# A graph layer on one core: 66 message buffers, one fetched tile in 36 split over two queues, three copies moved from ScalarE to VectorE, wider second tiles, and the last groups' products over fewer tiles

## The chip, the core and the metric

The kernel runs on one core of a Trainium2 chip. A core has TensorE (PE, whose loading of weights is shown as PEld), VectorE (DVE), ScalarE (ACT), GpSimd (POOL) and SyncE (SP), each with its own queue of instructions, and 16 DMA engines that all queues share. The metric is the device time of one execution in microseconds; lower is better. Most executions agree within 0.3%.

## What is computed

A graph of 12500 nodes with 256 features, and 212500 edges sorted by destination, each with a source, a destination and one of eight types. Node features are normalised and clipped at zero; each edge carries its source's features, multiplied by the weight of its type; messages are added up at their destination.

```
h = maximum(layernorm(x), 0)                        # 12500 x 256
hx = einsum('ni,rio->rno', h, weight)               # 8 types
agg = segment_sum(hx[edge_type, src], dst, 12500)
x + agg * sqrt(0.5) + h_bias + (h @ loop_weight) * sqrt(0.5)
```

Every node also has an edge to itself in the list. All values are float32.

## The kernel before

The kernel adds up first and multiplies after: for each destination node and type it sums the features `h` of the sources (`acc`), and then multiplies the sums of 128 nodes (a group, 98 in all) by the eight weights.

Edges are worked in *units*, 802 of them, each of two *tiles* of up to 128 edges, 1603 tiles in all. The first 128 units take 256 edges, later ones 267: the last edge of a node is its self edge where it appears so, and is left out of the tiles and added by the group's own path (`begin`, below). Block b is 128 units, whose indices are prepared together on VectorE.

For each tile t:

- `gather` (L742 to L760) fills a message buffer `msg[t]` (128 edges x 256) by an indirect DMA of POOL, one source row per partition. It is called 58 tiles (`AHEAD`) before the tile is used, into a ring of 60 buffers (`MSGS`). The first 96 tiles are gathered from `x`, while `h` is still being made, and are normalised in place: `moments` on DVE, and a pass of ACT (L716). The others are gathered from `h` in DRAM (`h32`).
- After block 0, one tile in 48 (`SINGLE`) is not gathered by POOL. `load_sources` (L762 to L773) loads 16 row addresses at a time into SP's registers (L765), and SP issues one DMA per row of 1 KB (L770). These steps stand in a list `fetches`, from which `fetch` takes four (`FETCH`) per tile, from eight tiles (`HOLD`) after the call on.
- `onehots` (L779) makes, for four tiles at a time, a 128 x 176 matrix per tile that says which of 22 nodes x 8 types an edge belongs to (L788). It runs 8 tiles (`LEAD`) ahead.
- `edge_sums` (L806) multiplies messages and one-hots on PE into one of four PSUM banks (L821): the first tile of a pair by 176 columns, the second, whose nodes are known to lie among the first 13 (`REACH`), by 104. In the profile each such product appears as two matmuls, so a tile has four.
- `add_sums` (L831) adds the bank of the pair before (L835, DVE) into a window of 22 nodes of `acc`, a ring of six groups of 128 nodes.

When a group's sums are complete (`plan.last`, worked out in `Plan` from bounds on where a unit's nodes can lie), its 18 products enter a queue that spreads them over the tiles up to `until`, at most some 16 tiles (L1012, 36 matmuls in the profile). `finish` (L1021) adds bias and products to the rows of x (L1024, L1025, DVE), and SP stores the rows for four groups at once (L1030), for the last two singly (L1027). SP also loads rows of x and h (L962).

The features of a group's own nodes are transposed on PE (L862) and copied by ACT to `self_t` (L867). For groups 12 and later `begin` writes them into `acc` by type (L884, eight DVE operations), and ACT's copy waits until these are done. The type of each node's self edge is found for four groups at once by `find_types`: ACT makes a diagonal matrix in four passes (L937), PE spreads it, ACT copies the result (L948).

The order of every engine is written out by the loop over tiles in `tile_preln_rgcn_kernel`: at tile t each step issues its instructions, and each engine runs its own in that order, waiting on semaphores. SP's stores and row fetches stand in one queue in that order.

Of the kernel before, what the change touches and what calls it, by code (L numbers as in the profile page):

```python
# [19 lines left out]
DVE = mybir.EngineType.DVE  # L20
SP = mybir.EngineType.SP

P = 128
# [11 lines left out]
WIN = 22  # L35
REACH = ((0, 13), (0, 22))

# [5 lines left out]

MSGS = 60
AHEAD = 58

SINGLE = 48
FETCH = 4
SOURCES = 16
HOLD = 8  # L50


QUAD = 4
LEAD = 8
PAIR = 2
# [4 lines left out]
DELAY = 6  # L60
REST = 3

BATCH = 4
# [16 lines left out]
class Plan:  # L80
# [7 lines left out]
    def __init__(self, N, E):  # L88
        U = PAIR * P
        first = P * U  # L90
        self.NU = NU = -(-E // U) if E <= first else P + -(-(E - first) // EDGES)
        self.EU = E - (NU - 1) * U if E <= first else E - first - (NU - P - 1) * EDGES
        self.NT = NU * PAIR - (1 if self.EU <= P else 0)
        self.rate = N / E * EDGES
        s = 6.5 * (E / 4) ** 0.5 + EDGES

        lines = [(U, 0), (EDGES, first - P * EDGES)]
        last = (1.1 * EDGES, 1.1 * (first - P * EDGES) - 0.1 * E - 1.5 * EDGES + s)
        self.low = [(a * N / E, (b - s) * N / E) for a, b in [*lines, last]]
# [16 lines left out]
        self.typed = min([q for q, b in enumerate(self.blocks) if b], default=len(self.blocks))  # L116
        assert XG * self.typed >= SLOTS
# [102 lines left out]
def kernel(  # L220
# [61 lines left out]
    with ExitStack() as main:  # L282
# [31 lines left out]
        added, zeroed = {}, {}  # L314
        single, fetches = {}, []
        state = {"h32": None}
# [425 lines left out]
        def gather(t):  # L742
# [18 lines left out]

        def load_sources(t, r0):  # L762

            b, _, u = place_of(t)
            _, vals = nc.values_load_multi_w_load_instructions(  # L765
                single[b][u : u + 1, r0 : r0 + SOURCES], engines=[SP],
                min_val=0, max_val=(N - 1) * D * 4,
                skip_runtime_bounds_check_because="clamped to the table where they are computed")
            for i, v in reversed(list(enumerate(vals))):
                fetches.insert(0, (0, lambda i=i, v=v: nc.sync.dma_start(  # L770
                    msg[t][r0 + i : r0 + i + 1, :].bitcast(U8),
                    h32_bytes[:, bass.ds(v, D * 4)])))
# [80 lines left out]

        def turn_nodes(g, pool, written=None):

# [9 lines left out]
            def keep():  # L865
                got["self", g] = pool.tile([P, KC, GROUP], F32, name="self_t")
                i = nc.scalar.activation(got["self", g][:, :, :n], pst[:, :, :n], AF.Copy)  # L867
                if written:
                    tc.add_manual_dep(
                        i.ins, written[0].name, SYNC_DEP, reason="one reader at a time")  # L870

            return turn, keep, pst

        def begin(g):

            n = plan.ends[g] - plan.starts[g]
            q, k = divmod(g, XG)
            written = []
            turn, keep, pst = turn_nodes(g, selves, written)
            s0 = g % SLOTS * GROUP  # L880

            def own(r):
                of = typed[q][:, k * GROUP : k * GROUP + n].unsqueeze(1).to_broadcast([P, KC, n])
                i = nc.vector.scalar_tensor_tensor(  # L884
                    acc[:, :, r, s0 : s0 + n], of, float(r + 1), pst[:, :, :n],
                    op0=ALU.is_equal, op1=ALU.mult)
                if r == R - 1:
                    zeroed[g, "slot"] = i.ins
                    written.append(i.ins)

# [19 lines left out]
        def find_types(q):  # L910
# [11 lines left out]
            def kinds_of():  # L922
# [11 lines left out]
                nc.vector.tensor_reduce(kinds, one, AX.X, ALU.add)  # L934
                marked[q] = marks.tile([P, XG * GROUP], BF16, name="diagonal")
# [32 lines left out]
        def group_ahead(g):  # L968
# [88 lines left out]
        with tc.manual_schedule():  # L1057
# [56 lines left out]
            def scale_weights():  # L1114
                for o in outs:
                    i = nc.vector.tensor_copy(o[:, 1, :], bias_in)
                done["bias"] = i.ins.name
# [41 lines left out]
            for t in range(NT):  # L1159
# [113 lines left out]
```

## Time and profile before

| | us |
|---|---|
| median of 3 runs (2019.54 to 2027.53) | 2020.34 |
| profiled execution | 2021.12 |
| its span | 2019.4 |
| PE busy / PEld / DVE | 1776.1 / 1585.9 / 1318.5 |
| ACT / POOL | 218.5 / 1497.1 |
| mean granted clock of PE | 0.951 |

A profile is one execution. "Busy" is the time in which an engine runs instructions; a group's line gives the count, the busy time, the mean of one in ns, and the idle time before its instructions with what ended it ("issue": nothing that the profile shows). In a timeline each line has the start, the duration, and in brackets the idle time before. In a view by stretch, the columns are the stretch, its length, the busy time of PE, PEld, DVE, ACT and POOL with counts, the granted clock, the DMA engines' busy share, and GB/s. In a view of one line the three durations are the least, the median and the greatest in ns. "SPq" and "ACTq" are the issuing queues of SP and ACT, whose DMA and register instructions do not count as busy.

### The profile page before, as it was taken

What the parts mean: (1) busy time and instruction counts of PE and PEld (TensorE: products, weight loads), DVE (VectorE), ACT (ScalarE), POOL (GpSimd) and SP (SyncE); (2) the same over time, 40 slices, a digit from 0 to 9 for tenths busy, and PEclk for the clock granted to TensorE, in tenths of its full rate; (3) what the DMA queues carried; (4) which work ended last, traced back from release to release, by engine and by line L of the source; (5) the groups of instructions that cost most, each with busy time, mean ns of one, the idle gap of its engine ahead of it and who ended that gap; (6) DMA issues with size and microseconds to landing.
All of it is one profiled execution on the core that took longest, in us unless ns stands there. A gap on an engine that the chain in (4) does not pass through costs nothing.

```text
span 2019.4 us, 36387 instructions
## 1 busy us (share of the span) xinstructions
PE 1776.1 (88%) x10411; PEld 1585.9 (79%) x10411; DVE 1318.5 (65%) x3282; ACT 218.5 (11%) x470; POOL 1497.1 (74%) x1602
## 2 busy tenths in 40 slices
PE   2458999998998898999998998898998898988998
PEld 2357999997888888888777777787787787877886
DVE  7869667687665578656577655578565568665642
ACT  7844110000000000000000000000000000000000
POOL 7757777777777777777777777777777777777773
PEclk8569999998999999999999999999999999999999
DMA  8963443444444444444444444444444444444442
GB/s 296 378 219 100 148 137 106 128 144 122 128 140 120 139 137 119 128 118 139 130 126 139 128 125 134 129 127 140 128 118 139 127 122 129 119 139 122 118 121 70
DMA packets 152577, 281.63 MB, mean 139 GB/s; under 512 B 31149, under 2 KB 101940, under 8 KB 152372
## 3 DMA queue, kind: packets, MB, share of 16 engines
q0 software_dynamic: 75648, 206.67, 34.6%
q1 hardware_dynamic: 76724, 72.61, 11.3%
q8 instruction: 82, 1.34, 0.3%
q14 instruction: 123, 1.01, 0.2%
HBM read 253.55 MB, written 25.60 MB: 138 GB/s over the span
## 4 chain that ended last, share of the span: by engine, by line
PE 36%; DMA 19%; SPq 15%; issue 13%; POOL 8%; DVE 5%; ACT 2%; DVEq 0%; ACTq 0%; POOLq 0%
PE ps L821 19%; PE po L1012 17%; DMA msg<-h,gidx 14%; SPq L770 11%; POOL msg L758 8%; SPq L765 3%; ACT xt L716 1%; DMA h<-xt 1%; DMA hr<-h 1%; DMA msg<-h 1%; DVE e_stats L704 1%; DVE acc L835 1%; DMA w<-in_L_gnn_weight_dram 1%; DVE oh L788 1%; DMA xr<-in_x_dram 1%
## 5 line engine op out<-in xcount | busy, mean ns | idle before, releaser
L758 POOL DMA_INDIRECT msg<-h,gidx x1480 | 1404.0, 949 | 464.9 <-issue 365.4
L821 PE MATMUL ps<-oh,msg 128*128 128x176 f32 (+1 forms) x6412 | 1127.6, 305 | 219.3 <-DMA msg<-h,gidx 88.3
L821 PEld LDWEIGHTS ps<-oh,msg 128*128 128x128 f32 x6412 | 1023.4, 197 | 377.5 <-DMA msg<-h,gidx 175.6
L1012 PE MATMUL po<-w,acc 128*128 128x256 f32 x3136 | 901.5, 390 | 0.7 <-DVE acc L835 0.7
L835 DVE TENSOR_TENSOR acc<-acc,ps 128x352 f32 x802 | 415.4, 518 | 496.2 <-PE ps L821 490.0
L1012 PEld LDWEIGHTS po<-w,acc 128*128 128x128 f32 x3136 | 538.1, 194 | 24.0 <-DVE acc L835 1.3
L788 DVE TENSOR_TENSOR oh<-fixed,cols 128x704 f32<-128x704 f32 x402 | 353.4, 880 | 0.0
L884 DVE SCALAR_TENSOR_TENSOR acc<-types,pt 128x256 f32<-128x256 bf16 (+1 forms) x688 | 249.4, 413 | 84.3 <-PE pt L862 79.3
L867 ACT ACTIVATE self_t<-pt 128x256 f32<-128x256 f32 x98 | 37.5, 383 | 1456.2 <-DVE acc L884 1387.8
L758 POOL DMA_INDIRECT msg<-in_x_dram,gidx x96 | 91.1, 949 | 31.0 <-issue 25.0
L1012 PE MATMUL po<-wl,self_t 128*128 128x256 f32 x392 | 107.8, 399 | 6.5 <-ACT self_t L867 2.6
L1012 PEld LDWEIGHTS po<-wl,self_t 128*128 128x128 f32 x392 | 70.0, 199 | 13.3 <-ACT self_t L867 3.0
L1024 DVE TENSOR_TENSOR xr<-xr,po 128x256 f32<-128x256 f32 x98 | 40.5, 413 | 18.2 <-PE po L1012 16.7
L716 ACT ACTIVATE xt<-xt,n_shift,n_rstd 128x256 f32<-128x256 f32 x98 | 50.9, 588 | 8.9 <-DVE n_shift L713 8.9
L716 ACT ACTIVATE msg<-msg,e_shift,e_rstd 128x256 f32<-128x256 f32 x96 | 49.6, 588 | 12.9 <-DVE e_shift L713 12.9
L1025 DVE TENSOR_TENSOR xr<-xr,po 128x256 f32<-128x256 f32 x98 | 41.2, 421 | 3.4
L937 ACT ACTIVATE diagonal<-ident,kinds 128x128 bf16<-128x128 f32 x88 | 28.1, 390 | 135.2 <-DVE kinds L934 130.7
L862 PE MATMUL pt<-ident,hr 128*128 128x128 f32 x196 | 38.4, 279 | 0.0
L371 DVE TENSOR_SCALAR moves<-fixed 128x267 int32<-128x267 int32 x84 | 36.0, 429 | 1.1
L704 DVE BATCH_NORM_STATS2 n_stats<-xt 128x6 f32<-128x256 f32 x98 | 34.4, 412 | 2.9 <-DMA xt<-in_x_dram 2.1
L372 DVE COPY_PREDICATED fixed<-moves,fixed 128x266 int32<-128x266 int32 (+6 forms) x84 | 33.7, 401 | 2.9
L704 DVE BATCH_NORM_STATS2 e_stats<-msg 128x6 f32<-128x256 f32 x96 | 33.5, 411 | 0.0
(201 smaller groups left out, 321.1 us busy)
## 6 DMA issues: line engine op xcount, KB each, us to landing
msg<-h SPq DMA_DIRECT2D x3456, 1.0 KB
msg<-h,gidx POOLq DMA_INDIRECT x1480
xt<-in_x_dram SPq DMA_DIRECT2D x24, 512.0 KB
h<-xt SPq DMA_DIRECT2D x24, 512.0 KB
xr<-in_x_dram SPq DMA_DIRECT2D x24, 512.0 KB
hr<-h SPq DMA_DIRECT2D x24, 512.0 KB
out_dram<-xr SPq DMA_DIRECT2D x24, 512.0 KB
w<-in_L_gnn_weight_dram SPq DMA_DIRECT2D x2, 1024.0 KB
```

The lines of the kernel that those rows point to most:

```text
L704: nc.vector.bn_stats(stats[:n, j, :], rows_[j])
L716: nc.scalar.activation(rows_[j], rows_[j], AF.Relu, bias=shift[:n, j : j + 1], scale=rstd[:n, j : j + 1])
L758: nc.gpsimd.indirect_dma_start(out=msg[t], out_offset=None, in_=table[:, :], in_offset=bass.IndirectOffsetOnAxis(ap=gidx[b][:, at : at + 1 ...
L765: _, vals = nc.values_load_multi_w_load_instructions(single[b][u : u + 1, r0 : r0 + SOURCES], engines=[SP], min_val=0, max_val=(N - 1) * D ...
L770: fetches.insert(0, (0, lambda i=i, v=v: nc.sync.dma_start(msg[t][r0 + i : r0 + i + 1, :].bitcast(U8), h32_bytes[:, bass.ds(v, D * 4)])))
L788: j = nc.vector.tensor_tensor(o[:, k : k + v, :i, :], iota_f.unsqueeze(1).unsqueeze(1).to_broadcast([P, v, i, C]), of.unsqueeze(3).to_broa ...
L821: j = nc.tensor.matmul(ps[:, c, :width], m[:, c * P : (c + 1) * P], o[:, :width], start=(i == 0 and c == 0), stop=(end and c == KC - 1))
L835: i = nc.vector.tensor_tensor(a, a, ps, op=ALU.add)
L884: i = nc.vector.scalar_tensor_tensor(acc[:, :, r, s0 : s0 + n], of, float(r + 1), pst[:, :, :n], op0=ALU.is_equal, op1=ALU.mult)
L1012: i = nc.tensor.matmul(got["out", g][:n], lhs, rhs, start=(r == R and c == 0), stop=(r == R - 1 and c == KC - 1))
L1024: nc.vector.tensor_add(rows_[:n, k, :], rows_[:n, k, :], outs[g % 2][:n, 1, :])
L1025: nc.vector.tensor_add(rows_[:n, k, :], rows_[:n, k, :], got["out", g][:n])
```

## The change

- The ring of message buffers has 66 instead of 60, and `AHEAD` is 64. Space for it comes from the bias (now in a row buffer), from two instead of three buffers of columns, and from one buffer of one-hots less.
- `LEAD` is 4 instead of 8: one-hots are made four tiles ahead.
- One tile in 36 is fetched row by row. Its rows 0 to 31 are issued by SP, the other 96 by ACT's queue; each loads 32 addresses at a time. Each engine has its own list, and three steps per tile are taken from each.
- The copies `self_t` and `types`, and the diagonal (now one operation), go to VectorE. The copy of `self_t` no longer waits for `begin`'s writes by a dependency, as one engine does both.
- The second tile of a pair covers 16 nodes, so 128 columns.
- The bound near the end of the edge list is another line, by which groups 84 to 96 count as complete one to three units earlier; the last eight groups (`SOON`) spread their products over at most six tiles (`DELAY`).

In the changed kernel POOL has 1568 gathers, of which 100 are from `x`; ACT has 3360 row DMAs and 105 loads of addresses, SP 1120 and 35.

```
-REACH = ((0, 13), (0, 22))
+REACH = ((0, 16), (0, 22))
-MSGS = 60
-AHEAD = 58
-
-SINGLE = 48
-FETCH = 4
-SOURCES = 16
+MSGS = 66
+AHEAD = 64
+
+SINGLE = 36
+FETCH = 3
+SOURCES = 32
-LEAD = 8
+LEAD = 4
+SOON = 8
-        last = (1.1 * EDGES, 1.1 * (first - P * EDGES) - 0.1 * E - 1.5 * EDGES + s)
+        last = (1.05 * EDGES, 1.05 * (first - P * EDGES) - 0.05 * E - 0.8 * EDGES + s)
-    bias_in = const.tile([P, D], F32, name="bias_in")
-        cols = main.enter_context(tc.tile_pool(name="cols", bufs=3))
+        cols = main.enter_context(tc.tile_pool(name="cols", bufs=2))
-        single, fetches = {}, []
+        single, fetches = {}, {SP: [], ACT: []}
...
-            if b and t % PAIR and kind[t] == "h" and t % SINGLE == SINGLE - 1 and t + AHEAD < NT:
-                for r in range(0, P, SOURCES):
-                    fetches.append((done["tile"] + HOLD, lambda r=r: load_sources(t, r)))
-                return
+            if b and t % PAIR and kind[t] == "h" and t + AHEAD < NT:
+                if t % SINGLE == SINGLE - 1:
+                    for k, r in enumerate(range(0, P, SOURCES)):
+                        engine = ACT if k else SP
+                        fetches[engine].append((
+                            done["tile"] + HOLD,
+                            lambda r=r, engine=engine: load_sources(t, r, engine)))
+                    return
...
-                single[b][u : u + 1, r0 : r0 + SOURCES], engines=[SP],
+                single[b][u : u + 1, r0 : r0 + SOURCES], engines=[engine],
...
+            queue = {SP: nc.sync, ACT: nc.scalar}[engine]
             for i, v in reversed(list(enumerate(vals))):
-                fetches.insert(0, (0, lambda i=i, v=v: nc.sync.dma_start(
+                fetches[engine].insert(0, (0, lambda i=i, v=v: queue.dma_start(
...
-            for _ in range(n):
-                if fetches and fetches[0][0] <= done["tile"]:
-                    fetches.pop(0)[1]()
+            for list_ in fetches.values():
+                for _ in range(n):
+                    if list_ and list_[0][0] <= done["tile"]:
+                        list_.pop(0)[1]()
...
-                i = nc.scalar.activation(got["self", g][:, :, :n], pst[:, :, :n], AF.Copy)
-                if written:
-                    tc.add_manual_dep(
-                        i.ins, written[0].name, SYNC_DEP, reason="one reader at a time")
+                nc.vector.tensor_copy(got["self", g][:, :, :n], pst[:, :, :n])
...
-                for g in range(XG):
-                    nc.scalar.activation(
-                        marked[q][:, g * GROUP : (g + 1) * GROUP], ident, AF.Copy,
-                        scale=kinds[:, g : g + 1])
+                nc.vector.tensor_tensor(
+                    marked[q].rearrange("p (g k) -> p g k", g=XG),
+                    ident.unsqueeze(1).to_broadcast([P, XG, GROUP]),
+                    kinds.unsqueeze(2).to_broadcast([P, XG, GROUP]), op=ALU.mult)
...
-                nc.scalar.activation(typed[q], pt, AF.Copy)
-
-            shared(spread, [(1, types_of)], lambda: q in marked, wait=2)
+                nc.vector.tensor_copy(typed[q], pt)
+
+            shared(spread, [(2, types_of)], lambda: q in marked, wait=2)
...
-                    shared(turn, [(1, keep)])
+                    shared(turn, [(2, keep)])
...
+                bias_in = got["bias"] = rowp.tile([P, XG, D], F32, tag="rows", name="biasr")[:, 0, :]
...
+                        if g >= plan.NG - SOON:
+                            until = min(until, ready + DELAY)
```

More of the change, by code (lines that the diff above doesn't have):

```diff
@@ L21 @@
 SP = mybir.EngineType.SP
+ACT = mybir.EngineType.Activation
 P = 128
@@ L760, in gather, with load_sources @@
                 in_offset=bass.IndirectOffsetOnAxis(ap=gidx[b][:, at : at + 1], axis=0))
-        def load_sources(t, r0):
+        def load_sources(t, r0, engine):
             b, _, u = place_of(t)
             _, vals = nc.values_load_multi_w_load_instructions(
-                single[b][u : u + 1, r0 : r0 + SOURCES], engines=[SP],
+                single[b][u : u + 1, r0 : r0 + SOURCES], engines=[engine],
                 min_val=0, max_val=(N - 1) * D * 4,
                 skip_runtime_bounds_check_because="clamped to the table where they are computed")
+            queue = {SP: nc.sync, ACT: nc.scalar}[engine]
             for i, v in reversed(list(enumerate(vals))):
-                fetches.insert(0, (0, lambda i=i, v=v: nc.sync.dma_start(
+                fetches[engine].insert(0, (0, lambda i=i, v=v: queue.dma_start(
                     msg[t][r0 + i : r0 + i + 1, :].bitcast(U8),
@@ L852, in clear, with turn_nodes @@
             zeroed[g, "slot"] = i.ins
-        def turn_nodes(g, pool, written=None):
+        def turn_nodes(g, pool):
             n = plan.ends[g] - plan.starts[g]
@@ L877, in begin @@
             q, k = divmod(g, XG)
-            written = []
-            turn, keep, pst = turn_nodes(g, selves, written)
+            turn, keep, pst = turn_nodes(g, selves)
             s0 = g % SLOTS * GROUP
@@ L888, in own @@
                     zeroed[g, "slot"] = i.ins
-                    written.append(i.ins)
             def write():
@@ L934, in kinds_of @@
                 nc.vector.tensor_reduce(kinds, one, AX.X, ALU.add)
-                marked[q] = marks.tile([P, XG * GROUP], BF16, name="diagonal")
-                for g in range(XG):
-                    nc.scalar.activation(
-                        marked[q][:, g * GROUP : (g + 1) * GROUP], ident, AF.Copy,
-                        scale=kinds[:, g : g + 1])
+                marked[q] = marks.tile(
+                    [P, 2, XG * GROUP], BF16, tag="mark0", name="diagonal")[:, 0, :]
+                nc.vector.tensor_tensor(
+                    marked[q].rearrange("p (g k) -> p g k", g=XG),
+                    ident.unsqueeze(1).to_broadcast([P, XG, GROUP]),
+                    kinds.unsqueeze(2).to_broadcast([P, XG, GROUP]), op=ALU.mult)
             shared(find, [(2, kinds_of)])
@@ L1115, in scale_weights @@
                 for o in outs:
-                    i = nc.vector.tensor_copy(o[:, 1, :], bias_in)
+                    i = nc.vector.tensor_copy(o[:, 1, :], got["bias"])
                 done["bias"] = i.ins.name
```

## The prediction

> **What bounds the kernel now.** The page's busy shares come first: PE 88%, POOL 74%, DVE 65%. A share doesn't say which engine sets the pace, so the second view is POOL's timeline. The instructions that gather message tiles are on L758.
>
> ```profile
> PE 1776.1 (88%) x10411; PEld 1585.9 (79%) x10411; DVE 1318.5 (65%) x3282; ACT 218.5 (11%) x470; POOL 1497.1 (74%) x1602
> L758 POOL DMA_INDIRECT msg<-h,gidx x1480 | 1404.0, 949 | 464.9 <-issue 365.4
> L758 POOL DMA_INDIRECT msg<-in_x_dram,gidx x96 | 91.1, 949 | 31.0 <-issue 25.0
> ```
>
> ```profile
> 4.72 1.11 POOL L758 DMA_INDIRECT msg<-in_x_dram,gidx  x1 [2.08 <-DVE bound_o L1088]
> ...
> 128.86 0.94 POOL L758 DMA_INDIRECT msg<-h,gidx  x1 [0.30 <-issue]
> 134.98 0.94 POOL L758 DMA_INDIRECT msg<-h,gidx  x1 [5.18 <-ACT e_rstd L708]
> 136.23 0.95 POOL L758 DMA_INDIRECT msg<-h,gidx  x1 [0.30 <-issue]
> 142.96 0.94 POOL L758 DMA_INDIRECT msg<-h,gidx  x1 [5.79 <-issue]
> ...
> 188.83 0.94 POOL L758 DMA_INDIRECT msg<-h,gidx  x1 [2.73 <-issue]
> ...
> 1992.75 0.95 POOL L758 DMA_INDIRECT msg<-h,gidx  x1 [0.30 <-PE ps L821]
> ```
>
> A gather takes 0.95 us and the next follows 0.30 us later, whoever is named as releaser: 1.25 us each. From 4.72 to 1992.75 there are 1576; 1575 x 1.25 = 1969 of the 1988 us. About 13.7 us of the rest are stalls at 129 to 195 us (5.18, 5.79, 1.02, 2.73, 0.49, each less the usual 0.30). So POOL's chain of gathers sets the time, and 26.6 us follow the last one's start. The chain of waits names PE and SPq before 947 us, but POOL's gaps stay at 0.30 there, so I go by the gaps.
>
> Third, busy time by stretch, columns PE, PEld, DVE, ACT, POOL:
>
> ```profile
> 300.00:350.00 50.00, 50.00 (x325) 47.27 (x325) 34.62 (x76) 4.18 (x11) 37.82 (x41) 1.00 0.37 106
> 550.00:600.00 50.00, 46.44 (x291) 43.33 (x290) 30.63 (x66) 3.03 (x8) 37.85 (x40) 0.97 0.45 131
> 750.00:800.00 50.00, 46.49 (x297) 43.41 (x295) 43.87 (x116) 2.64 (x7) 37.81 (x41) 0.99 0.42 122
> ```
>
> Until about 450 us PE is full: it works off the backlog of the start. Later it has gaps, and POOL's 40 or 41 gathers per 50 us stay.
>
> Fourth, the queue that fetches one tile in 48 row by row, and loads of its addresses:
>
> ```profile
> 1559.78 41.06 SPq L770 DMA_DIRECT2D msg<-h  x101
> L765 SPq TENSOR_LOAD <-single x216: 1146/1261/2742, 292.8 to 1897.8; - x108
> L632 ACTq TENSOR_LOAD <-flag x1: 468/468/468, 1770.3 to 1770.3; - x1
> L632 SPq TENSOR_LOAD <-flag x1: 542/542/542, 1781.6 to 1781.6; - x1
> 911.45 1.50 DMA msg<-h
> ```
>
> A row costs the queue 0.32 us (101 rows and seven loads of 1.3 in 41.06), and lands 1.83 us after its instruction starts (911.12 to 912.95 on the chain).
>
> **The change, part by part.** *One tile in 36.* Fetched are tiles t with t % 36 = 35, block 1 or later, t + 64 < 1603: 287 to 1511, so 35, where it was 27 (287 to 1535). POOL issues 1568 gathers: 8 x 1.25 = **10.0 us** off its chain.
>
> *66 buffers.* A gather reuses the buffer of the tile 66 before it instead of 60. Its stalls come from PE releasing pairs late: gathers 100, 102, 104, 136 and 140 waited for the pairs 60 back, released at 134.7, 142.7, 145.9, 188.5 and 193.7. The same releases now hold gathers 106, 108, 110, 142 and 146, which without a stall come 7.5 us later. Stepping through them leaves 0, 2.9, 0.7, 2.7 and 0.2 us = 6.5 instead of 13.7. Against it: 100 tiles instead of 96 come unnormalised (four more bn_stats at 0.41 and ACT passes at 0.59), but behind tile 80; the pair 96/97 has some 8 us to spare. DVE, full at 150 to 200 us (47.72 of 50), gets three or four early copies (1.7 us) and, with the shorter lead, one one-hot less (0.88): 0.8 us later. Gain 13.7 - 6.5 - 0.8 = **6.4 us**; bounds 0 (releases as much later) and 7.5.
>
> *ACT's copies on DVE.* 98 self copies from PSUM, 128x256: a DVE copy from `pt` of that size (L352) takes 0.424, so 41.6 us. 22 diagonals and 22 type copies, 128 x 512: no such DVE row. Lines through 256 elements at 0.424 and 704 at 0.88 give 0.69; the conversion L905 has 0.49. I take 0.69: 30 us. In all 72 us of DVE on 1318. They lie in DVE's waits for PE (490 us on L835); where DVE is fullest (43.87 of 50 at 750) they add 1.8. A PE stall there is won back later, as a PE pair has slack (below). The path pays 0; bounds 0 and, if every one held POOL's next gather, 72.
> At 750 to 800 us POOL starts as many gathers as at 550, with 13 us more DVE work beside it, so I take 0. The Trainium skill ("SBUF — State Buffer", section "SBUF: two separate sides", the "DVE blocks DMA" trap) says that a VectorE operation holding the port shared with GpSimd keeps a gather's descriptors from being written; by it the moved copies could cost up to those 72 us. The rows above speak against it for this kernel's mix, and the same page limits the trap to two-port or two-SBUF-input operations.
>
> *16 columns of nodes in the second tile.* 3072 matmuls grow from 104 to 128 columns. On the chain four of 104 take 0.42 us, four of 176 0.60: 0.0025 per column, +0.06 per pair. A pair of tiles costs PE 0.60 + 0.42 + 2.2 products (98 x 18 / 802) at 0.43 + 0.05 of transposes = 2.02 us, now 2.08; POOL needs 2 x 1.25 x 35/36 = 2.43. Cost 0, bounds 0 and 768 x 0.06 = 46 if PE were the bound.
>
> *One-hots four tiles ahead.* Same number and width. PE may run six tiles ahead of DVE's order instead of ten; while it waits for each gather, it does not. So 0; bounds 0 and 98, the time PE waited for the adds of L835 so far (51.1 + 46.8), were as much put on the path.
>
> *SP 32 rows, ACT 96.* Each DMA of either queue raises one of eight completion semaphores in turn and waits until its last use has landed. While SP's 32 and ACT's rows alternate, each queue has four in flight: 1.9 / 4 = 0.475 us a row; ACT's other 64 have all eight, and with SP's price 0.32. A load of 32 addresses: 0.54 for one, 1.26 for 16, so 2.03. ACT's round is 32 x 0.475 + 64 x 0.32 + 3 x 2.03 = 41.8, and SP's large transfers on the same semaphores (36.4 us of waits of L770 in 27 rounds) add 1.0: 42.8 us, against 35 x 1.25 = 43.75 us per 36 tiles. It fits narrowly. Behind ACT's rows is queued nothing, since its copies are gone; PE waits for them. A fetch is issued from 56 to 23 tiles ahead, 28 us of cover; during PE's catching up (1.0 us a tile, tiles 287 to 345) some 11 us of it go. SP's output stores wait for DVE, and through the semaphores hold ACT back to that order, not further. So 0. What no row shows is a row's price on ACT. A one-address load is no slower there (0.47 against 0.54), so I take 0.32; bounds 0.29 (0.32 less SP's move of 0.03) and 0.41 (0.32 and once more the rest beside the 0.23 of the instruction itself).
>
> *The last groups.* Product 96 is ready a unit earlier, and eight groups spread over at most six tiles. Before, PE ended the last tile at 2004.8, some 8 us after it landed at 1996.7; the last group's products started at 2006.4 and ended at 2014.4 = landing + 17.7. Now the order has 13 tiles and 36 products from tile 1590 on, which PE reaches without backlog: 13 x 0.60 + 36 x 0.43 - 0.65 = 22.6 us after that landing, and the last lands 15.0 after it, so + 7.6; 1.0 for the add, hiding the two self products, 16 x 0.43: + 15.5. Then the 5.0 us as before. Gain 2.2, with the wait for the output buffer gone up to 3: **2.6 us**; bounds 0 and 6 (no queue at PE).
>
> The bias in a row buffer and two column buffers: that slot's store was issued five pieces earlier; 0.
>
> Sum: 10.0 + 6.4 + 2.6 = 19.0. Span 2019.4 - 19.0 = 2000.4; the profiled execution took 2021.1, 1.7 above its span, and 0.8 above the median. So 2002 us.
>
> **Rivals.**
> 1. *ACT's fetches set the pace (slower).* If a row costs ACT more, each 0.01 adds 0.64 us to a round. Over 33 rounds the cover left (17 us) and what PE wins back over the last 91 tiles (91 x 0.175 = 16 us) allow 33 us of lag: a round of 44.75, or 0.35 us a row. At 0.36 the gain is used up; at 0.40 a round is 47.9 and the time 2002 + 33 x 4.15 - 33 = 2106. For it: 42.8 of 43.75 is nearly full, and SP already came late 14 times (72 us of waits of PE for `msg<-h`). Against it: the load on ACT, and that a late tile costs nothing until the cover is gone.
> 2. *Only the gathers are saved.* PE releases later by what the buffers give, the tail stays: 2021.1 - 10.0 = 2011; with half of it 2006. For it: DVE is full just there. Against it: the releases at 135 to 146 come before any moved copy.
> 3. *PE or DVE becomes the bound.* 46 us of wider matmuls, or 72 of DVE work, on the path, less 19.0: 2048 or 2074. Against: 0.35 us of slack per pair, DVE below 44 of 50.
> 4. *The port rule*, the moved copies holding POOL one by one: 2021.1 + 72 - 19.0 = 2074 at most. The windows speak against it.
>
> **How the numbers follow.** Forecast 0.53 (1994 to 2007); rival 2 0.15 (2004 to 2012, mostly still faster); rival 1 mild, 0.35 to 0.36 a row, 0.10 (2008 to 2030), strong 0.15 (to 2106); rivals 3 and 4 0.07. A measurement of this kernel tells about 0.5%, 10 us, from no change. Faster 0.66, same 0.13, slower 0.21. The range goes from 1994 (6 us of tail) to 2045, which takes in rival 1 to about 0.37 a row.
>
> **What would show it.** Right: 1568 gathers still 1.25 us apart, gaps at 130 to 195 us summing to some 7 us, the last starting near 1976, ACT's rows 0.32 to 0.48 apart. Wrong: PE waiting for `msg<-h` more and more as the run goes on, POOL gaps over 0.3 us after 200 us, gathers longer than 0.95 us.

## The result: 14% slower, and the profile after

The changed kernel takes 2300.85 us (median of 4 runs, 2296.73 to 2303.66), the kernel before beside it 2019.94. The ratio is 1.138, with a 95% interval from 1.1352 to 1.1408; the forecast was 2002, with a range up to 2045. The profiled execution took 2303.66, its span 2301.9. Four of the six groups of runs below were made where the kernel before took 2569 to 2596 us instead of 2020 (the expectations call it the slow chip), and results from there are given as ratios to the kernel before measured beside them; the changed kernel itself was not run there.

The page of the changed kernel: busy shares, the chain that ended last by engine, and the groups of the gathers and of the edge sums (L763 and L828 are L758 and L821 of the kernel before).

```profile
PE 1764.4 (77%) x10411; PEld 1637.0 (71%) x10411; DVE 1374.3 (60%) x3434; ACT 142.5 (6%) x267; POOL 1492.4 (65%) x1594
PE 35%; DMA 23%; ACTq 23%; issue 8%; DVE 6%; SPq 2%; ACT 2%; DVEq 0%
L763 POOL DMA_INDIRECT msg<-h,gidx x1468 | 1395.6, 951 | 693.5 <-issue 369.8
L828 PE MATMUL ps<-oh,msg 128*128 128x176 f32 (+1 forms) x6412 | 1126.6, 309 | 517.0 <-DMA msg<-h 440.4
```

No engine is nearly full any more, and PE, VectorE and POOL have no more to do than forecast. A gather still takes 0.95 us. What is new is ACTq with 23% of the chain and 440 us in which PE's edge sums wait for rows of `msg` that were fetched one by one (48.7 us before). The waits of PE and POOL, and those of SP's queue, are these (what waited, for what, us in total, times, longest):

```profile
PE ps L828 <- DMA msg<-h: 440.4, 34, 20.5
POOL msg L763 <- PE ps L828: 285.1, 171, 14.5
```

```profile
SPq L776 <- DMA msg<-h: 572.3, 298, 24.5
SPq L1033 <- DMA msg<-h: 275.0, 18, 35.2
```

Thirty-four times, once for each fetched tile after the first, PE stands still for 6 to 20 us. The busy time by stretch (PE, PEld, DVE, ACT, POOL) shows it beside the three stretches of before: where PE had 46.5 of 50 us and POOL 40 or 41 gathers, there are now 38 to 39 us, and later 34 gathers.

```profile
300.00:350.00 50.00, 50.00 (x324) 47.28 (x323) 37.32 (x84) 0.00 (x0) 37.80 (x40) 1.00 0.37 107
550.00:600.00 50.00, 39.27 (x247) 36.53 (x247) 27.44 (x60) 0.00 (x0) 37.80 (x41) 0.88 0.38 109
750.00:800.00 50.00, 38.46 (x230) 36.05 (x231) 30.77 (x72) 0.00 (x0) 31.27 (x34) 0.83 0.33 94
```

POOL falls back only after the message buffers have filled up. Its timeline shows how: gathers 1.25 us apart, then a gap for a buffer that PE has not released.

```profile
1021.39 0.95 POOL L763 DMA_INDIRECT msg<-h,gidx  x1 [0.30 <-issue]
1033.26 0.94 POOL L763 DMA_INDIRECT msg<-h,gidx  x1 [10.92 <-PE ps L828]
1034.50 0.95 POOL L763 DMA_INDIRECT msg<-h,gidx  x1 [0.30 <-issue]
1037.96 0.94 POOL L763 DMA_INDIRECT msg<-h,gidx  x1 [2.51 <-PE ps L828]
```

So the rows on ACT's queue set the pace. They are not dear in themselves. In the views of the two lines that issue rows (L776) and load addresses (L770), durations are the least, the median and the greatest in ns:

```profile
L776 ACTq DMA_DIRECT2D msg<-h x3360: 213/213/561, 334.9 to 2177.3; - x198
L776 SPq DMA_DIRECT2D msg<-h x1120: 224/228/997, 334.9 to 2103.5; - x187
```

```profile
L770 ACTq TENSOR_LOAD <-single x105: 2154/2292/2487, 252.8 to 2164.7; - x105
```

Rows that ACT issues without a wait start 0.31 us apart; I had taken 0.32. A load of 32 addresses takes 2.29 us; I had 2.03. A round is the work from one fetched tile to the next. From the first row to the last, 334.9 to 2177.3 us, 35 rounds take 52.6 us each. I split that by adding up in the trace what ACT's queue did: 30.2 us of rows, 6.8 of address loads, and 15.6 of waits, of which 5.5 stand before the landing of a row of SP, 3.7 before an output store of SP, 3.2 before ACT's own rows, and the rest mostly before SP's loads of x and h. A round may take 43.75. I had forecast 42.8, with 6.0 us in it for all waits.

### The profile page after: what moved, and what is told of

Same layout as the page of the kernel before. It is cut to its first block, busy times and chain, and to the rows that moved or that the text cites. A ratio compares the mean times of both kernels' runs of the same rounds, so it can differ in the third digit from the quotient of the medians.

```text
span 2301.9 us, 38182 instructions
## 1 busy us (share of the span) xinstructions
PE 1764.4 (77%) x10411; PEld 1637.0 (71%) x10411; DVE 1374.3 (60%) x3434; ACT 142.5 (6%) x267; POOL 1492.4 (65%) x1594
## 4 chain that ended last, share of the span: by engine, by line
PE 35%; DMA 23%; ACTq 23%; issue 8%; DVE 6%; SPq 2%; ACT 2%; DVEq 0%
ACTq L776 19%; PE ps L828 18%; PE po L1015 16%; DMA msg<-h 13%; DMA hr<-h 4%; DMA xr<-in_x_dram 4%; ACTq L770 4%; SPq L776 2%; DVE acc L842 1%; ACT xt L717 1%; DVE oh L795 1%; DVE e_stats L705 1%; DMA h<-xt 1%; DMA w<-in_L_gnn_weight_dram 1%; DMA out_dram<-xr 0%
## 5 line engine op out<-in xcount | busy, mean ns | idle before, releaser
L763 POOL DMA_INDIRECT msg<-h,gidx x1468 | 1395.6, 951 | 693.5 <-issue 369.8
L828 PE MATMUL ps<-oh,msg 128*128 128x176 f32 (+1 forms) x6412 | 1126.6, 309 | 517.0 <-DMA msg<-h 440.4
L828 PEld LDWEIGHTS ps<-oh,msg 128*128 128x128 f32 x6412 | 1059.0, 202 | 608.1 <-issue 289.6
L1015 PEld LDWEIGHTS po<-w,acc 128*128 128x128 f32 x3136 | 547.7, 197 | 29.0 <-DVE acc L842 2.0
L763 POOL DMA_INDIRECT msg<-in_x_dram,gidx x100 | 94.9, 949 | 32.3 <-issue 26.2
L717 ACT ACTIVATE xt<-xt,n_shift,n_rstd 128x256 f32<-128x256 f32 x98 | 50.9, 588 | 9.1 <-DVE n_shift L714 9.1
L874 DVE COPY self_t<-pt 128x256 f32<-128x256 f32 x98 | 40.6, 415 | 3.2 <-PE pt L869 3.2
L951 DVE CAST types<-pt 128x512 bf16<-128x512 f32 x22 | 15.2, 689 | 23.8 <-PE pt L947 23.6
```

Source lines behind the costliest of these rows:

```text
L717: nc.scalar.activation(rows_[j], rows_[j], AF.Relu, bias=shift[:n, j : j + 1], scale=rstd[:n, j : j + 1])
L763: nc.gpsimd.indirect_dma_start(out=msg[t], out_offset=None, in_=table[:, :], in_offset=bass.IndirectOffsetOnAxis(ap=gidx[b][:, at : at + 1 ...
L828: j = nc.tensor.matmul(ps[:, c, :width], m[:, c * P : (c + 1) * P], o[:, :width], start=(i == 0 and c == 0), stop=(end and c == KC - 1))
L874: nc.vector.tensor_copy(got["self", g][:, :, :n], pst[:, :, :n])
L1015: i = nc.tensor.matmul(got["out", g][:n], lhs, rhs, start=(r == R and c == 0), stop=(r == R - 1 and c == KC - 1))
```

## The experiments

### Everything but the split fetch

```
-SINGLE = 36
-FETCH = 3
-SOURCES = 32
+SINGLE = 48
+FETCH = 4
+SOURCES = 16
...
-                        engine = ACT if k else SP
+                        engine = SP
```

> The changed kernel with the row fetch of the kernel before: one tile in 48, all rows by SP, 16 addresses at a time, four steps per tile. All else is as changed: 66 buffers, copies on VectorE, lead of 4, 128 columns, the end. Theory A: 2009 to 2013, as nothing but the split fetch is at fault. Theory C: near 2300. If one of the other parts costs a little by itself, 2015 to 2030.

> The changed kernel with the row fetch of the kernel before put back (one tile in 48, all 128 rows by SyncE, 16 addresses to a load); all other parts stay. Its first trial stood at 0.998 of the kernel before on a chip where that takes 2573 us. Theory A (the fetch that is split between SyncE and ScalarE is the whole loss, the other parts are harmless): on a chip where the kernel before takes 2020 us, 2008 to 2015: less the 6.4 us of start stalls, as many gathers as before. Rival B (copies on VectorE and 128 columns are a part of the loss): 2030 or more, ratio above 1.005.

The first took 2570.89 against 2572.78, ratio 0.998 (0.994 to 1.001). The second took 2011.06 us against 2020.11, ratio 0.9957 (0.9944 to 0.9971): theory A. The wider second tiles, the moved copies, the shorter one-hot lead, the 66 buffers and the new end together gain 9 us. The whole loss needs the new way in which the one tile is fetched.

### The split fetch alone

The kernel before, with the split fetch and the copies on VectorE, which the split needs to leave ACT's queue free:

```
-SINGLE = 48
-FETCH = 4
-SOURCES = 16
+SINGLE = 36
+FETCH = 3
+SOURCES = 32
...
+                        engine = ACT if k else SP
```

> The kernel before with the split fetch (one tile in 36, 32 rows by SyncE, 96 by ScalarE) and the copies on VectorE alone; 60 message buffers, 104 columns and the one-hot lead as before. Theory A (the split fetch is the whole loss): 2290 to 2330 where the kernel before takes 2020, as much as the changed kernel or some us more, since the fetched tile's buffer comes 6 tiles later; TensorE waits for message rows in every round of 36, some 440 us. Rival B (the loss needs the 128 columns or the shorter one-hot lead as well): 2050 to 2150.

2359.34 us, ratio 1.1672 (1.1655 to 1.169); PE waits 34 times, 496.5 us, for fetched rows. Theory A holds and rival B falls, but the number is 29 us above the range, and 58 us above the changed kernel. Up to 9 of these may be the gain of the other parts, which this kernel lacks; the rest goes with 60 buffers instead of 66. A tile fetched six tiles later explains six tiles once, not some 50 us. That was the first sign that the number of buffers is part of a loop which is run through in every round.

### Without SP's output stores

```
-                elif k == XG - 1:
-                    first = plan.starts[XG * q]
-                    nc.sync.dma_start(
-                        out[first : d0 + n].rearrange("(k p) d -> p k d", p=P), rows_)
```

> The changed kernel without SP's stores of the output rows of groups 0 to 95 (its output holds only the last two groups); everything is still computed. In the changed kernel ACT's rows wait 129 us for these stores on the shared semaphores, 16 times some 8 us, and 194 us for rows of SP, part of which stand behind such a store. Theory A with these waits as the main loss: a round falls from 52 to between 46.5 (129 us and half of the 194 gone) and 49, and the time to 2301 - 35 x (3.5 to 6) = 2090 to 2180. If the waits only move to the next transfer: above 2250.

> The changed kernel without SyncE's stores of the first 96 groups, so that those rows of the output are never written. In the changed kernel ScalarE stood 129 us of its 547 us of waits for those stores. Theory A1 (the stores are a term of their own in ScalarE's round): 2150 to 2190 where the kernel before takes 2020. Rival A2 (ScalarE's wait for a store stands beside its wait for SyncE's rows, and the next late one takes its place): 2250 to 2300.

A single run each: 2635.53, 1.024 of the kernel before at 2573; and 2196.29 us beside 2020, 6 us above A1's range and 54 below A2's. The stores cost the changed kernel about 105 us of its 281.

### Without SP's rows

```
-                        engine = ACT if k else SP
-                        fetches[engine].append((
-                            done["tile"] + HOLD,
-                            lambda r=r, engine=engine: load_sources(t, r, engine)))
+                        if k:
+                            fetches[ACT].append((
+                                done["tile"] + HOLD,
+                                lambda r=r: load_sources(t, r, ACT)))
+                        else:
+                            fetches[SP].append((
+                                done["tile"] + HOLD,
+                                lambda: nc.sync.dma_start(msg[t][:SOURCES, :], h32[:SOURCES, :])))
```

> The changed kernel with SyncE's 32 rows of a fetched tile left out: one transfer brings 32 fixed rows of the table in their place, so a quarter of each fetched tile's messages is not the right one. ScalarE's 96 rows and its three address loads stay, as do SyncE's stores. Theory A (ScalarE's 194 us of waits for SyncE's rows are a term of their own): 2301 - 194 = 2107, 2090 to 2130. Rival A2 (the next late transfer, a store or a row of its own, takes their place): 2200 to 2280. Rival A3 (SyncE, rid of rows that wait for ScalarE's, also brings its stores earlier, and the waits for those go too): 2010 to 2060.

> The changed kernel with SyncE's 32 rows of a fetched tile left out (one transfer of 32 fixed rows in their place, so a quarter of each fetched tile's messages is not the right one), ScalarE's 96 rows, its address loads and SyncE's stores kept, on a chip where the kernel before takes 2020. Theory A (the 194 us that ScalarE stood for SyncE's rows are a term of their own): 2090 to 2130. Rival A2 (another late transfer takes their place): 2200 to 2280. Rival A3 (SyncE, without rows that wait for ScalarE's, brings its stores earlier, and the waits for those go too): 2010 to 2060. On the slow chip the same kernel stood at 1.017.

1.017 beside a kernel before at 2569; 2221.16 us beside 2021, 80 us less than the changed kernel. That is rival A2. By the trace, ACT's some 190 us before SP's 32 rows have become 160 us before SP's single transfer, 26 waits of up to 16 us, and its waits before SP's loads of h have grown from 27 to 85 us. Taking 31 of 32 transfers away hardly shortens the first of these, so it is no matter of their number: ACT waits for the moment at which SP's first transfer may start.

### One tile in 48, still split

```
-SINGLE = 36
+SINGLE = 48
```

> The changed kernel with one fetched tile in 48 instead of 36 and nothing else altered: 27 fetched tiles, rows still 32 by SP and 96 by ACT. Theory A (the rate): a round of ACT's queue takes some 52 us (3360 rows from 334.9 to 2177.3 us are 35 rounds of 52.6), and it is late only because 35 gathers of POOL take 43.75; 47 gathers take 58.75, so PE stops waiting, POOL is the bound again, and the time is 2021 less 9 (the stalls at the start, 13.7 before and 4.7 in the changed kernel) less 2 to 3 at the end: 2009 to 2013. Theory B (the order): rows by ACT come late by their place behind SP's stores on the shared completion semaphores, however far apart the tiles are; then each of 27 tiles still holds PE by 7 to 20 us and the time stays above 2150. Theory C (the rest of the change: copies on VectorE, shorter lead): near 2300.

> The changed kernel with one tile in 48 fetched in place of one in 36, still 32 rows by SyncE and 96 by ScalarE. Theory A (a round of some 52 us is too long only for the 43.75 that 35 gathers leave): 52 to 55 us against 58.75, TensorE's waits for fetched rows under 100 us, 2005 to 2015 where the kernel before takes 2020. Rival B (the waits between the two queues grow with the time they have, since each waits for buffers and stores that the other work sets): round 60 or more, 2060 to 2100, as the ratio of 1.03 on the chip where the kernel before takes 2573 would have it.

> The changed kernel with one tile in 48 fetched in place of one in 36, still 32 rows by SyncE and 96 by ScalarE, on a chip where the kernel before takes 2020. Theory A (a round of 52 to 55 us is too long only for the 43.75 that 35 gathers leave; 47 leave 58.75): 2005 to 2020, TensorE's waits for fetched rows under 100 us. Rival B (ScalarE's waits grow with the time between two tiles, since they are waits for stores and buffers that the other work sets): round 60 or more, 2060 to 2100.

1.030 and 1.029 beside a kernel before at 2573 and 2569; 2104.28 us beside 2021, ratio 1.0409 (1.0391 to 1.0426). Theory A falls, and the number is just above rival B's range. A round has 15 us more, and ACT's waits grow from 15.6 to 25 us, so that it still comes out too long, at 62 us. My sum of rows, loads and waits can't explain that. The chain of waits can.

### The loop that the chain shows

One round of the changed kernel in the chain of waits, in order of time (start, us, what); the pieces left out are further rows of the same queues and PE's products:

```profile
559.00 1.19 PE ps L828 x4
...
566.80 0.46 PE ps L828 x4
567.27 0.27 SPq L776
567.66 0.23 SPq L776
567.99 2.02 DMA msg<-h
570.02 1.62 DMA msg<-h
...
581.02 1.97 DMA msg<-h
583.01 0.21 ACTq L776
...
590.74 2.30 ACTq L770
...
603.08 0.21 ACTq L776
603.39 1.82 DMA msg<-h
605.56 1.19 PE ps L828 x4
```

At 559.00 PE gets its fetched tile, call it T. Eight microseconds later its edge sums release SP's first row, which belongs to tile T + 72: that row's buffer was last used by the tile 66 before it, T + 6, so PE had six tiles to work through. SP's 32 rows alternate with rows of ACT that belong to T + 36, and in the compiled order of transfers those stand behind them: the two queues raise the same eight completion semaphores in turn, and these are given out in the order of the compiled program. That order is not the source's. By the numbers of its instructions the source issues ACT's rows of tile 647 while tiles 590 to 622 are worked, and SP's rows of the next fetched tile, 683, after them, at 626 to 636; in the compiled program ACT's rows stand at tiles 615 to 646, up to the tile itself, and SP's rows of 683 in between, at 617 to 632. At 583.01 ACT has passed SP's last row; its remaining rows and one address load take 20 us; at 605.56 PE gets T + 36. PE releases SP, SP releases ACT, ACT releases PE. The 64 tiles by which fetches are called ahead are no cover in this loop, since it goes through a buffer that is free only six tiles after T.

Measured over all rounds in which PE waited, from instruction times in the trace (us):

| kernel | tiles to go, 2 x SINGLE - MSGS | PE resumes to SP's first row | SP's 32 rows | to ACT's last row | sum |
|---|---|---|---|---|---|
| changed kernel | 72 - 66 = 6 | 12.0 | 14.9 | 24.0 | 50.9 |
| split alone, 60 buffers | 72 - 60 = 12 | 17.1 | 14.5 | 20.8 | 52.5 |
| without the stores | 6 | 9.5 | 13.9 | 24.7 | 48.1 |
| one transfer by SP | 6 | 10.8 | 0 | 37.5 | 48.3 |
| one in 48, split | 96 - 66 = 30 | 35.8 | 15.6 | 8.8 | 60.2 |

The first term follows the tiles to go at about a microsecond a tile: 5.1 us for six more, 23.8 for 24 more. The loop of the kernel with 60 buffers is 1.6 us longer, and 34 x 1.6 = 54, where it lost some 50 to 58. In the kernel with a single transfer by SP the loop is 2.6 us shorter, 34 x 2.6 = 88, and it took 80 us less: there some 83 of ACT's 96 rows are still behind that transfer. The same piece of the chain in the kernel with 60 buffers and in that with one tile in 48:

```profile
567.56 1.16 PE ps L828 x4
...
581.48 1.03 PE ps L828 x8
582.53 0.26 SPq L776
...
594.16 2.11 DMA msg<-h
596.29 0.21 ACTq L776
```

```profile
773.72 1.19 PE ps L828 x4
...
802.83 2.08 PE ps L828 x16
804.91 0.23 PE pt L869 x2
...
805.31 0.23 SPq L776
...
816.46 1.52 DMA msg<-h
818.00 0.45 ACTq L776
```

15 and 32 us from PE's first product to SP's first row, where the changed kernel had 8 in the round shown. (Of the 32 rounds behind its 12.0, 24 have 8 to 11 us and the other eight 13 to 25. In seven of the eight an output store stood in SP's queue ahead of the row, in one a load of indices.) That is why twelve more tiles a round did not help: they lengthen its first part by 24 tiles' work, 23.8 us, while ACT, which gets further before it must wait, saves 15.2 at the end. It is also why the stores cost 105 us: they wait in SP's queue ahead of SP's rows, for landings of ACT's rows and then for VectorE, and in the loop without them 2.8 us are missing, 34 times 2.8 being 95. All these terms were read from runs already made; the kernels that follow were run before I had them.

### The rows halved

```
-                        engine = ACT if k else SP
+                        engine = ACT if k > 1 else SP
```

> The changed kernel with the 128 rows halved, 64 by SyncE and 64 by ScalarE. By the trace of the changed kernel 64 rows and two address loads are 64 x 0.31 + 2 x 2.29 = 24.4 us on ScalarE; with its 15.6 us of waits in a round 40.0, under the 43.75 that a round of 35 gathers leaves. Theory A (the length of ScalarE's round decides): 2000 to 2030 where the kernel before takes 2020, TensorE's wait for message rows under 100 us. Rival C (ScalarE's waits grow with SyncE's share, since its rows stand between more of SyncE's on the shared semaphores): round of 45 to 50, 2060 to 2200.

2000.7 us (1999.35 to 2000.99), ratio 0.9902 (0.9887 to 0.9917): theory A's number, and 1% faster than the kernel before; rival C falls. PE no longer waits for fetched rows, and POOL's line of them is eight times its usual 0.3 us:

```profile
POOL msg L763 <- DMA msg<-h: 2.4, 8, 0.3
```

In the first rounds, with PE still behind, ACT started its rounds 35 to 38 us apart, and its waits there were for its own rows and SP's transfers, hardly any for PE. That is below the 43.75 that POOL leaves, so the loop does not close on PE. (In the compiled order it is now SP's rows that end at the tile itself, for tile 647 at tiles 614 to 646, and ACT's stand at 590 to 622.) The sum of ACT's own round foretold this result too, so this run doesn't tell the loop from that sum; one tile in 48 does.

One tile in 32 with the rows halved was run three times, each beside a kernel before at 2569 to 2596:

```
-SINGLE = 36
+SINGLE = 32
...
-                        engine = ACT if k else SP
+                        engine = ACT if k > 1 else SP
```

> The changed kernel with the rows halved (64 by each queue) and one tile in 32 fetched. Some 39 fetched tiles instead of 35: 4 or 5 gathers fewer, 5 to 6 us. Theory A (rounds were 36 to 38 us where nothing held them, against the 38.75 that 31 gathers leave): 1994 to 1998 where the kernel before takes 2020. Rival B (a round with an output store in it is longer than 38.75): 2005 to 2040, with TensorE waiting for fetched rows in every second round.

> The changed kernel with the rows halved and one tile in 32 fetched, on a chip where the kernel before takes 2020; on the slow chip it stood at 0.986. 1563 gathers against 1568 of the half split at 36 (2000.7 us): 5 x 1.25 = 6 us less. Theory A (64 rows leave each queue room at 38.75 us a round): 1993 to 1998. Rival B (rounds with an output store come out over 38.75): 2001 to 2040, TensorE waiting for fetched rows in many rounds.

> The changed kernel with the rows halved and one tile in 32 fetched, on a chip where the kernel before takes 2020. Theory A (64 rows leave each queue room at 38.75 us a round; 5 gathers fewer than at 36, 6 us): 1993 to 1998. Rival B (rounds with an output store come out over 38.75): 2001 to 2040, TensorE waiting for fetched rows in many rounds. On the slow chip it stood at 0.985.

Ratios of 0.986, 0.984 and 0.985, each interval below 0.99, where SP alone at one in 48 had 0.998. PE waited for fetched rows once or twice in each, 2 to 4 us in all, so rival B's sign is not there. It beats the kernel before under this condition; the forecast times were for the other one, and whether it beats the halved rows at one in 36 was not measured.

### The shares exchanged, and other variants

```
-                        engine = ACT if k else SP
+                        engine = SP if k else ACT
```

> The changed kernel with the two shares exchanged: 96 rows by SyncE, 32 by ScalarE, one tile in 36. In the compiled order the long share stands at the same places as before (its last row just ahead of the tile's use). SyncE's round: 96 x 0.32 + 3 x 2.21 = 37.3 us, and waits. Theory A (ScalarE loses its time to transfers of the other queue, SyncE's stores and rows; a queue that carries the stores itself waits less for them: 197 us in 27 rounds of 48, 7.3 a round, where SyncE alone fetched): 5.5 to 7 us of waits, round 43 to 44.5, 2000 to 2040 where the kernel before takes 2020. Rival B (the waits come with 96 rows so close ahead of their use, whichever queue carries them): round of 50 or more, 2250 to 2320.

> The changed kernel with the shares exchanged, 96 rows by SyncE and 32 by ScalarE, one tile in 36, on a chip where the kernel before takes 2020. Theory A (ScalarE loses its time to SyncE's transfers; SyncE, with its stores in its own queue, does not): round of 43 to 45 us, 2000 to 2040. Rival B (the waits come with 96 rows so close ahead of their use, whichever queue carries them): round of 50 or more, 2250 to 2320.

Ratios of 1.066 and 1.069 (1.0646 to 1.0743), both beside a kernel before at 2594 to 2596, so the times expected for 2020 were not put to the test. What the trace tells is the order: in the loop read as above with the queues exchanged, PE resumes to ACT's first row 10.4 us, ACT's 32 rows 14.3, to SP's last row 35.0. The first two terms are near those of the changed kernel, 12.0 and 14.9, so the loop is there too when the queues are exchanged. The third is 11 us longer than 24.0. SP's register moves, which were slow there (below), make 4 of these and seven more rows some 2; the rest is not explained.

All 128 rows on ACT, one tile in 48:

```
-SINGLE = 36
-FETCH = 3
+SINGLE = 48
+FETCH = 4
...
-                        engine = ACT if k else SP
+                        engine = ACT
```

> The changed kernel with one tile in 48 fetched, all 128 rows of it by ScalarE; SyncE fetches no rows. Rows and address loads by the trace of the changed kernel: 128 x 0.31 + 4 x 2.29 = 48.9 us a round, 58.75 to be had. Theory A (what lengthens ScalarE's round is that its rows alternate with SyncE's): its waits without those for SyncE's rows, 547 - 194 = 353 us in 35 rounds, are 10.1 us, and at 128 rows and 48 tiles some 12 to 13: round 61 to 62, 2020 to 2060 where the kernel before takes 2020. Rival B (ScalarE's queue waits as much whatever SyncE fetches): 15.6 x 48 / 36 = 20.8 us of waits, round 70, 27 rounds of 11 us more: 2250 to 2300.

Ratio 1.058 (1.053 to 1.063), against 0.998 for the same rows on SP. ACT waited there 135 us for SP's stores and 57 us for SP's loads of h, so a queue that fetches alone is held too by transfers of the other; what that costs where the kernel before takes 2020 stays open.

Rows called eight tiles sooner:

```
-HOLD = 8
+HOLD = 0
```

> The changed kernel with the fetch's steps allowed eight tiles earlier (HOLD 0 instead of 8). Theory A: the rate is the same, so only some 10 us of cover are added once: 2285 to 2300. Theory B: a row that is issued eight tiles earlier (8 x 1.25 = 10 us) comes up to 10 us less late each time, 34 times: below 2100.

2711.87 against 2572.78, a single run, 1.054. The loop is there too (10.6, 17.8 and 29.8 us), so the earlier call is no cure. The compiled program fits that: the source now issues ACT's rows of tile 647 at tiles 582 to 614, but they still stand at 615 to 646, and SP's rows of 683 at 617 to 632. What the edit changes in time can't be said without the changed kernel under the same condition, and neither theory was put to the test.

## Why the prediction was wrong

- *The bound, one tile in 36, the gathers.* Right. With the rows halved, all other parts of the change in place and nothing late, 1568 gathers run 1.25 us apart; the last starts at 1976.11 (forecast near 1976), the span is 1998.9 (forecast 2000.4). Against SP alone at one in 48 the eight gathers fewer gave 10.4 us (forecast 10.0).
- *66 buffers and the end.* Together 6.4 + 2.6 = 9.0 forecast; SP alone with these and the harmless parts gained 9.05. That the two meet so closely is in part luck, for each part was forecast too small. In that kernel's profile the stalls of the start are 4.9 us instead of 13.7, and the end after the last gather's start is 22.8 instead of 26.6: 12.6 us, of which 1.6 are lost to small gaps of POOL later and the rest shows in the span (2019.4 to 2008.3). In the changed kernel the stalls were 4.9 us as well, not 6.5 + 0.8, as POOL's timeline shows (idle times in brackets, each with the usual 0.30).

```profile
147.46 0.95 POOL L763 DMA_INDIRECT msg<-h,gidx  x1 [1.30 <-PE pt L869]
184.81 0.94 POOL L763 DMA_INDIRECT msg<-h,gidx  x1 [1.30 <-issue]
192.50 0.94 POOL L763 DMA_INDIRECT msg<-h,gidx  x1 [2.99 <-ACT e_rstd L709]
195.21 0.94 POOL L763 DMA_INDIRECT msg<-h,gidx  x1 [0.52 <-issue]
```

- *Copies on VectorE.* 72 us of DVE forecast, 40.6 + 15.2 + 15.2 = 71.0 measured, none of it on the path. The three groups in the changed kernel:

```profile
L874 DVE COPY self_t<-pt 128x256 f32<-128x256 f32 x98 | 40.6, 415 | 3.2 <-PE pt L869 3.2
L939 DVE TENSOR_TENSOR diagonal<-ident,kinds 128x512 bf16<-128x512 f32 x22 | 15.2, 693 | 0.8
L951 DVE CAST types<-pt 128x512 bf16<-128x512 f32 x22 | 15.2, 689 | 23.8 <-PE pt L947 23.6
```

  Rival 4 is settled with it: the gathers took 949 ns before and 950 in the kernel that has these copies and SP's fetch, and that kernel gained what was forecast.

```profile
L763 POOL DMA_INDIRECT msg<-h,gidx x1476 | 1402.4, 950 | 454.2 <-issue 358.7
```

  The Trainium skill ("SBUF — State Buffer", section "SBUF: two separate sides", the "DVE blocks DMA" trap) warns of VectorE operations in a two-port mode that keep GpSimd from writing descriptors; no such cost shows for these copies, and whether they run in that mode no run shows.
- *128 columns, one-hots four ahead.* Nothing, as forecast: PE waited 46.8 us for the adds before and in the kernel with SP's fetch alike. In busy time the 3072 wider matmuls took 505.8 us in that kernel instead of 487.4, 18 more, where the bound was 46.
- *SP 32 rows, ACT 96.* Here the prediction failed. The prices of a row and of a load were nearly right (0.31 for 0.32, 2.29 for 2.03), so rival 1, which hung on the row's price, named the right place and the wrong reason. Three statements were wrong. "SP's large transfers ... add 1.0" and the alternation before it came to 6.0 us a round; ACT's waits were 15.6. "Through the semaphores [they] hold ACT back to that order, not further": but that order holds SP's rows of the tile after next, whose buffer PE frees six tiles past the tile it has just waited for. And "a fetch is issued from 56 to 23 tiles ahead, 28 us of cover": that is the order of the source, while the semaphores follow the compiled program, where ACT's rows stand from 31 tiles ahead to the tile itself. I counted a round as a sum of one queue's work; it is a loop through three queues, 50.9 us and 1.4 more until PE goes on. The cover was small from the start: ACT's last row of the first fetched tile starts at 393.3 and PE reaches that tile at 400.1; the second tile holds PE until 454.4, where the kernel with halved rows has it at 437.2, a lag of 17 us. From there to the last fetched tile, at 2179.1, PE takes 33 rounds of 52.3 us; with halved rows it is there at 1866.7, after rounds of 43.3. These 33 rounds lose 295 us, and of the 16 us that PE was to win back behind the last it wins 9: 303 us of span.

What stays open: that the split fetch is the loss, runs with and without it show; the loop as its mechanism was read from runs that had been made, its terms fit the five kernels of the table, and no kernel was built afterwards to break it at another place, for instance with the rows of both queues in the order of the source. Why the compiled order differs from the source is open. How the exchanged shares and one tile in 32 do where the kernel before takes 2020 was not measured.

## What to carry to other kernels

When a queue's work is split over two, don't add up each queue's own instructions: follow one round of the chain across both, through what each waits for, until it comes back to where it began. A lead of many tiles is worth only what the tightest place on that way leaves, here 2 x 36 - 66 = 6 tiles, because one queue's early rows stood in line ahead of the other's late ones. Take the order in which two queues share semaphores from the compiled program, not from the source. An even split of the rows turned a loss of 14% into a gain of 1%.

## What was not expected of the hardware

The same kernel, SP's fetch with the other parts of the change, ran with a span of 2008.3 us in one group and 2549.7 in another. POOL and VectorE were busy as long: 1499.2 and 1500.0 us, 1375.1 and 1371.9, and a gather took 0.95. PE was busy 1776.6 and 1934.6 us, at a granted clock of 0.951 and 0.885, which is far less than the difference of 541 us. In the longer one 274 of 1575 gathers start over 1.9 us after the one before, mostly some 2.65, where the other has three, and SP's register moves take 103 ns in the mean instead of 29, though the median stays at 29. POOL's timeline there:

```profile
1515.75 0.95 POOL L763 DMA_INDIRECT msg<-h,gidx  x1 [0.30 <-issue]
1518.55 0.94 POOL L763 DMA_INDIRECT msg<-h,gidx  x1 [1.85 <-remote]
1519.79 0.95 POOL L763 DMA_INDIRECT msg<-h,gidx  x1 [0.30 <-issue]
```

POOL stands still between instructions for something that the profile does not name ("remote"). The cause is unknown. The record has the same chip number, 4, for one of the four groups and one of the other two, so the name slow chip is not borne out. The loads of addresses were also new to me: on ACT 0.47 us for one value and 2.29 for 32, on SP 0.54, 1.26 for 16 and 2.21 for 32, so 0.05 to 0.06 us a value.
